# Transformer attention software-pipelined by the order of issue: scores of unit i+2 ahead of the values and sums of unit i

## The chip, the cores and the metric

One core of one Trainium2 chip runs the whole program. The metric is the device time of one execution in microseconds (us). A profile of one execution stands beside the timed runs. In it PE is TensorE's matmuls, PEld its weight loads, DVE is VectorE, ACT ScalarE, SP the queue that issues transfers. The ends of matmuls are modelled, so I read distances between starts ("pitches") rather than lengths. The granted clock is the share of TensorE's full speed that the profile shows as granted; 1.00 is full.

## The reference, cut to what matters

Two graph-attention layers, then one transformer layer on 4096 rows of 256 features, 8 heads of 32, with a 4096 x 4096 adjacency of 0 and 1 as mask. Only the attention of the last layer is touched:

```python
scores = jnp.einsum('nhd,mhd->hnm', q, k) * SCALE
scores = jnp.where(mask, scores, -jnp.inf)
attn = jax.nn.softmax(scores, axis=-1)
out = jnp.einsum('hnm,mhd->nhd', attn, v).reshape(n, DIM)
```

The kernel computes exp(scores) x mask without a shift, sums values and weights, and divides at the end; a flag would start a safe version if a sum left a wide range.

## The kernel before

A "unit" is one block of 512 query columns (nb), one half of the heads (c, four heads) and one tile of 128 keys (mt): 8 x 2 x 32 = 512 units. `HC` is 4, `O` 32, `NT` 32, `NB` 512, `MC` 8. I call the tiles `u_ps` score tiles (they lie in PSUM, where PE writes) and the tiles `u_e` weight tiles; a "turn" is the time from the first score of one unit to the first score of the next. In the traces, scores read `feat_a` and `feat_b`, the names of the tiles behind `q_t` and `k_t`.

```python
masks = tile_pool("u_masks", bufs=5);  work = tile_pool("u_work", bufs=6)
tail = tile_pool("u_tail", bufs=2)
ps_s = tile_pool("u_ps_s", bufs=3, space=PSUM)      # 2 banks each
ps_a = tile_pool("u_ps_a", bufs=1, space=PSUM)      # u_av, u_dn: 1 bank each
for nb in range(NNB):
    for k in range(NT // MC):                       # mask: load, turn into 0 and 1
        b = masks.tile([P, MC, NB], BF, name="u_mask")
        nc.sync.dma_start(b, v_cols[nb, :, k * MC : (k + 1) * MC, :])
        nc.vector.tensor_scalar(b, b, 0.0, None, op0=ALU.not_equal)
        ...
    for c in range(DC):
        av, dn = ...
        for mt in range(NT):
            ps = [ps_s.tile([P, 2, NB], F32, name="u_ps") for _ in range(HC // 2)]
            for j in range(HC):                     # scores: four row groups of the array
                nc.tensor.matmul(ps[j // 2][:, j % 2, :], k_t[...], q_t[...])
            for u in range(HC // 2):
                e = work.tile([P, 2, NB], F32, name="u_e")
                nc.scalar.activation(e, ps[u], AF.Exp)
                nc.vector.tensor_tensor(e, e, mask, op=ALU.mult)
            for to, left in ((av, None), (dn, ones)):
                for j in range(HC):                 # values, then sums: four column groups
                    nc.tensor.matmul(to[j * O : (j + 1) * O, :], ..., es[j // 2][:, j % 2, :],
                                     start=(mt == 0), stop=(mt == NT - 1))
        nc.scalar.copy(num, av);  nc.vector.tensor_copy(den, dn)
        ...                                         # store den
        nc.vector.reciprocal(inv, den)
        nc.vector.tensor_tensor(q_t[:, c, cols], num, inv, op=ALU.mult)
```

A scheduler that runs before the program is built fixes the order of instructions on each engine; it may differ from the order of the source.

## Time and profile before

| | before |
|---|---|
| timed median, 3 runs | 11645.31 us (11637.78 to 11648.66) |
| profiled span | 11641.4 us |
| attention stage, from its first scores to its last values and sums | 3494.5 us, 6.83 us a unit |
| granted PE clock in this stage | 0.90 |

The prediction below shows the slices (each digit the busy tenths of one fortieth of the span), the stage's window, its waits (engine and line, what it waited for, us in total, times, longest) and one turn of the timeline (start, length, engine, instruction; in square brackets the idle time before it and what ended it). What to see: no engine is full, and three waits recur in every unit. That is a ring.

### The profile page before, as it was taken

To read this page: it belongs to the slowest core of one execution; us is meant where nothing else is said; L and a number is where in the kernel's file an instruction comes from. 1 tells how busy PE (TensorE), PEld (TensorE's weight loads), DVE (VectorE), ACT (ScalarE), POOL (GpSimd) and SP (SyncE) were. 2 spreads that over 40 slices of the span, in tenths; PEclk is the share of its full clock that TensorE was granted. 3 is DMA by queue.
4 is the path that set the end of the run, shared out by engine and by line. 5 is a ranking of instruction groups with operands and counts; after the bars stand their busy time and mean duration, and the time that the engine had idled before them with its cause. 6 is when DMAs were issued, how large, how long until landed. Compare 5 with 4: busy or idle time off the path is not lost.

```text
span 11641.4 us, 101805 instructions
## 1 busy us (share of the span) xinstructions
PE 9711.6 (83%) x40040; PEld 3205.0 (28%) x40546; DVE 7718.6 (66%) x8204; ACT 5333.2 (46%) x7825; POOL 36.1 (0%) x47
## 2 busy tenths in 40 slices
PE   7888999999999888899999999966666666666669
PEld 4333322222222333332222222221111111111125
DVE  7999877777777899977777777733333333333331
ACT  1101288888888100038888888822222222222221
POOL 0000000000000000000000000000000000000000
PEclk8999999999999899999999999989988988988989
DMA  3232100000000100000000000000000000000000
GB/s 96 80 81 79 47 15 15 15 15 14 12 11 4 49 26 29 29 4 17 17 17 17 17 17 11 7 18 8 8 15 8 8 15 8 8 15 8 4 16 22
DMA packets 116850, 262.66 MB, mean 23 GB/s; under 512 B 12933, under 2 KB 87942, under 8 KB 91782
## 3 DMA queue, kind: packets, MB, share of 16 engines
q1 hardware_dynamic: 111750, 222.46, 5.5%
q0 software_dynamic: 4608, 33.56, 1.5%
q8 instruction: 319, 5.23, 0.2%
q14 instruction: 173, 1.42, 0.0%
HBM read 213.92 MB, written 75.50 MB: 25 GB/s over the span
## 4 chain that ended last, share of the span: by engine, by line
PE 62%; DVE 24%; ACT 6%; issue 6%; DMA 1%; SPq 0%; DVEq 0%; ACTq 0%; POOLq 0%
PE av L185 20%; DVE part L170 14%; PE u_av L859 9%; PE ps L375 8%; PE ps L382 7%; PE u_dn L859 7%; DVE u_e L852 5%; PE u_ps L840 5%; ACT u_e L850 4%; DVE e L405 2%; PE misc L359 2%; PE misc L949 1%; PE misc L935 1%; DMA v<-in_adj_dram 1%; ACT e L408 1%
## 5 line engine op out<-in xcount | busy, mean ns | idle before, releaser
L408 ACT ACTIVATE e<-e,terms 128x512 f32<-128x512 f32 x4096 | 2627.2, 709 | 458.3 <-DVE e L405 448.3
L405 DVE TENSOR_TENSOR e<-e,ps 128x1024 f32<-128x1024 f32 x2048 | 2450.3, 1218 | 274.2 <-PE ps L382 172.4
L852 DVE TENSOR_TENSOR u_e<-u_e,u_mask 128x1024 f32<-128x1024 f32 x1024 | 1208.0, 1221 | 2146.0 <-ACT u_e L850 2145.9
L185 PE MATMUL av<-e,v_sb 128*64 128x512 f32 x8192 | 2547.6, 617 | 52.7 <-ACT e L408 47.9
L170 DVE TENSOR_REDUCE part<-ps_peak 128x2 f32<-128x1024 f32 x2048 | 2328.2, 1216 | 69.5 <-PE ps_peak L274 63.5
L859 PE MATMUL u_av<-u_e,u_v 128*32 128x512 f32 x4096 | 1254.9, 781 | 1158.2 <-DVE u_e L852 1158.2
L850 ACT ACTIVATE u_e<-u_ps 128x1024 f32<-128x1024 f32 x1024 | 990.7, 1021 | 2448.9 <-PE u_ps L840 2448.9
L375 PE MATMUL ps<-bias,ident 128*128 128x512 bf16 x4084 | 1557.6, 381 | 186.8 <-DVE e L405 160.6
L390 ACT ACTIVATE e<-slope,steep 128x512 f32<-128x512 f32 x2048 | 1405.8, 712 | 343.4 <-PE av L185 335.5
L397 DVE TENSOR_SCALAR e<-slope,steep 128x512 f32<-128x512 f32 x2048 | 969.6, 483 | 792.6 <-PE av L185 756.1
L167 PE MATMUL ps_peak<-v,ident 128*128 128x512 bf16 x3997 | 1223.0, 386 | 292.7 <-DVE v L148 104.5
L382 PE MATMUL ps<-shift,select 128*128 128x512 bf16 x3784 | 1441.4, 381 | 1.6 <-issue 1.4
L274 PE MATMUL ps_peak<-dst_rows,select 128*128 128x512 bf16 x4013 | 1223.6, 385 | 5.9 <-issue 0.4
L859 PE MATMUL u_dn<-u_e,u_ones 128*32 128x512 f32 x4096 | 1140.2, 683 | 0.0
L185 PEld LDWEIGHTS av<-e,v_sb 128*64 128x64 f32 x8192 | 554.9, 134 | 1089.6 <-ACT e L408 983.6
L382 PEld LDWEIGHTS <-select 128*128 128x128 bf16 x4096 | 398.1, 97 | 1231.5 <-issue 975.6
L375 PEld LDWEIGHTS <-ident 128*128 128x128 bf16 x4096 | 398.5, 97 | 1149.7 <-issue 905.4
L167 PEld LDWEIGHTS <-ident 128*128 128x128 bf16 x4096 | 393.8, 99 | 994.6 <-issue 666.0
L840 PE MATMUL u_ps<-feat_a,feat_b 32*128 32x512 f32 x4096 | 617.3, 639 | 5.9 <-ACT u_e L850 5.4
L859 PEld LDWEIGHTS u_av<-u_e,u_v 128*32 128x32 f32 x4096 | 162.7, 120 | 1653.3 <-DVE u_e L852 1581.3
L289 ACT COPY stage<-pv 128x1024 bf16<-128x1024 bf16 x128 | 129.2, 1013 | 1041.5 <-PE pv L288 1041.5
L134 ACT COPY shift<-pr 17x1024 bf16<-17x1024 bf16 x8 | 7.6, 1000 | 1203.0 <-PE pr L133 1202.8
(132 smaller groups left out, 3734.4 us busy)
## 6 DMA issues: line engine op xcount, KB each, us to landing
bias<-v_cols SPq DMA_DIRECT2D x64, 1024.0 KB, 4.9
v<-in_adj_dram POOLq DMA_DIRECT2D x32, 1024.0 KB, 7.7
v_rows<-v SPq DMA_DIRECT2D x32, 1024.0 KB, 3.8
v_cols<-stage SPq DMA_DIRECT2D x16, 2048.0 KB, 8.9
v<-v_rows SPq DMA_DIRECT2D x32, 1024.0 KB, 4.8
u_mask<-v_cols SPq DMA_DIRECT2D x32, 1024.0 KB, 4.8
feat_b<-in_x_dram SPq DMA_DIRECT2D x8, 512.0 KB, 8.0
x_spill<-feat_a SPq DMA_DIRECT2D x8, 512.0 KB, 3.0
```

The lines of the kernel that those rows point to most:

```text
L167: nc.tensor.matmul(ps[:, j, :], ident, v[:, cols], start=True, stop=False)
L170: nc.vector.tensor_reduce(part[:, 2 * hp : 2 * hp + 2, w], ps, AX.X, ALU.max)
L185: nc.tensor.matmul(av[2 * O * j : 2 * O * (j + 1), :], v_sb[:, mt, VW * (h // 2) + O * (h % 2) : VW * (h // 2) + O * (h % 2) + 2 * O], p, ...
L274: nc.tensor.matmul(ps, select[:, h, :], dst_rows[:, cols], start=False, stop=True)
L375: nc.tensor.matmul(ps[:, j, :], ident, chunks[mt // MC][:, mt % MC, :], start=True, stop=False,)
L382: nc.tensor.matmul(ps[:, j, :], select[:, h, :], shift[:, cols], start=False, stop=True,)
L390: nc.scalar.activation(e[:, j, :], slope[:, j, :], AF.Relu, bias=steep[:, mt, h : h + 1],)
L405: nc.vector.tensor_tensor(e, e, ps, op=ALU.add)
L408: nc.scalar.activation(e[:, j, :], e[:, j, :], AF.Exp, bias=terms[:, mt, H + h : H + h + 1],)
L850: nc.scalar.activation(e, ps[u], AF.Exp)
L852: nc.vector.tensor_tensor(e, e, mask.unsqueeze(1).to_broadcast([P, 2, NB]), op=ALU.mult)
L859: nc.tensor.matmul(to[j * O : (j + 1) * O, :], v_sb[:, mt, h * O : (h + 1) * O] if left is None else left[:, :O], es[j // 2][:, j % 2, :], ...
```

## The change

The intent is to break the ring without another buffer or instruction. The loop body is split in two. `weights` issues a unit's scores, exponentials and mask products; `weigh` issues its values and sums. Two units of scores stay ahead.

```diff
-                for mt in range(NT):
-                    ps = [...]            # scores, exponentials, products
-                    ...
-                    for to, left in ((av, None), (dn, ones)):   # values and sums, same unit
-                        ...
+        def weights(nb, c, mt):           # scores, exponentials, products
+            if c == 0 and mt == 0:
+                load_masks(nb)
+            ...
+            return es
+        def weigh(nb, c, mt, es):         # values and sums; after mt == NT - 1 the division
+            ...
+        units = [(nb, c, mt) for nb in range(NNB) for c in range(DC) for mt in range(NT)]
+        pending = []
+        for unit in units:
+            pending.append((*unit, weights(*unit)))
+            if len(pending) > 2:
+                weigh(*pending.pop(0))
+        for unit in pending:
+            weigh(*unit)
```

More of the change, by code (lines that the diff above doesn't have):

```diff
@@ L825, in unshifted_transformer, with block_cols, load_masks @@
         ps_a = scope.enter_context(tc.tile_pool(name="u_ps_a", bufs=1, space=PSUM))
-        for nb in range(NNB):
-            cols = slice(nb * NB, (nb + 1) * NB)
+        masks_of = {}
+        sums_of = {}
+        def block_cols(nb):
+            return slice(nb * NB, (nb + 1) * NB)
+        def load_masks(nb):
             chunks = []
@@ L833, in unshifted_transformer @@
                 chunks.append(b)
-            for c in range(DC):
-                av = ps_a.tile([P, NB], F32, name="u_av")
-                dn = ps_a.tile([P, NB], F32, name="u_dn")
-                for mt in range(NT):
-                    ps = [ps_s.tile([P, 2, NB], F32, name="u_ps") for _ in range(HC // 2)]
-                    for j in range(HC):
-                        nc.tensor.matmul(
-                            ps[j // 2][:, j % 2, :],
-                            k_t[j * O : (j + 1) * O, c, mt * P : (mt + 1) * P],
-                            q_t[j * O : (j + 1) * O, c, cols],
-                            start=True,
-                            stop=True,
-                        )
-                    es = []
-                    for u in range(HC // 2):
-                        e = work.tile([P, 2, NB], F32, name="u_e")
-                        nc.scalar.activation(e, ps[u], AF.Exp)
-                        mask = chunks[mt // MC][:, mt % MC, :]
-                        nc.vector.tensor_tensor(
-                            e, e, mask.unsqueeze(1).to_broadcast([P, 2, NB]), op=ALU.mult
-                        )
-                        es.append(e)
-                    for to, left in ((av, None), (dn, ones)):
-                        for j in range(HC):
-                            h = c * HC + j
-                            nc.tensor.matmul(
-                                to[j * O : (j + 1) * O, :],
-                                v_sb[:, mt, h * O : (h + 1) * O] if left is None else left[:, :O],
-                                es[j // 2][:, j % 2, :],
-                                start=(mt == 0),
-                                stop=(mt == NT - 1),
-                            )
-                num = tail.tile([P, NB], F32, name="u_num")
-                den = tail.tile([P, NB], F32, name="u_den")
-                nc.scalar.copy(num, av)
-                nc.vector.tensor_copy(den, dn)
-                for j in range(HC):
-                    at = (nb * DC + c) * HC + j
-                    nc.sync.dma_start(dens[at : at + 1, :], den[j * O : j * O + 1, :])
-                inv = tail.tile([P, NB], F32, name="u_inv")
-                nc.vector.reciprocal(inv, den)
-                nc.vector.tensor_tensor(q_t[:, c, cols], num, inv, op=ALU.mult)
@@ new lines, in load_masks @@
+            masks_of[nb] = chunks
+        def weights(nb, c, mt):
+            if c == 0 and mt == 0:
+                load_masks(nb)
+            ps = [ps_s.tile([P, 2, NB], F32, name="u_ps") for _ in range(HC // 2)]
+            for j in range(HC):
+                nc.tensor.matmul(
+                    ps[j // 2][:, j % 2, :],
+                    k_t[j * O : (j + 1) * O, c, mt * P : (mt + 1) * P],
+                    q_t[j * O : (j + 1) * O, c, block_cols(nb)],
+                    start=True,
+                    stop=True,
+                )
+            es = []
+            mask = masks_of[nb][mt // MC][:, mt % MC, :]
+            for u in range(HC // 2):
+                e = work.tile([P, 2, NB], F32, name="u_e")
+                nc.scalar.activation(e, ps[u], AF.Exp)
+                nc.vector.tensor_tensor(
+                    e, e, mask.unsqueeze(1).to_broadcast([P, 2, NB]), op=ALU.mult
+                )
+                es.append(e)
+            return es
@@ new lines, in weigh @@
+        def weigh(nb, c, mt, es):
+            if mt == 0:
+                sums_of[nb, c] = (
+                    ps_a.tile([P, NB], F32, name="u_av"),
+                    ps_a.tile([P, NB], F32, name="u_dn"),
+                )
+            av, dn = sums_of[nb, c]
+            for to, left in ((av, None), (dn, ones)):
+                for j in range(HC):
+                    h = c * HC + j
+                    nc.tensor.matmul(
+                        to[j * O : (j + 1) * O, :],
+                        v_sb[:, mt, h * O : (h + 1) * O] if left is None else left[:, :O],
+                        es[j // 2][:, j % 2, :],
+                        start=(mt == 0),
+                        stop=(mt == NT - 1),
+                    )
+            if mt < NT - 1:
+                return
+            num = tail.tile([P, NB], F32, name="u_num")
+            den = tail.tile([P, NB], F32, name="u_den")
+            nc.scalar.copy(num, av)
+            nc.vector.tensor_copy(den, dn)
+            for j in range(HC):
+                at = (nb * DC + c) * HC + j
+                nc.sync.dma_start(dens[at : at + 1, :], den[j * O : j * O + 1, :])
+            inv = tail.tile([P, NB], F32, name="u_inv")
+            nc.vector.reciprocal(inv, den)
+            nc.vector.tensor_tensor(q_t[:, c, block_cols(nb)], num, inv, op=ALU.mult)
```

## The prediction

> **What bounds the kernel now.** I read, in this order: the slices of the span, the chain that ended last, the waits, and the timeline of single units. The slices show three stages with different limits:
>
> ```profile
> PE   7888999999999888899999999966666666666669
> ...
> DVE  7999877777777899977777777733333333333331
> ACT  1101288888888100038888888822222222222221
> ...
> PEclk8999999999999899999999999989988988988989
> ```
>
> The last third (about slice 27 to 39) is the transformer's attention, the only code that the change touches. No engine is full there: PE 6 tenths, DVE 3, ACT 2. A stage without a full engine is bound by a chain. The window that covers it alone gives its size:
>
> ```profile
> 7770.00:11264.50 3494.50, 2330.44 (x12288) 617.26 (x12288) 1311.47 (x1101) 1001.40 (x1042) 0.16 (x1) 0.90 0.03 10
> ```
>
> The columns are length, then busy time of PE, PEld, DVE, ACT and POOL, then granted clock. The stage has 512 units (8 column blocks x 2 halves x 32 key tiles), so one costs 3494.5 / 512 = 6.83 us, with only 2.56 us of DVE and 1.96 us of ACT. The waits of this window name the ring:
>
> ```profile
> ACT u_e L850 <- PE u_ps L840: 2448.9, 496, 9.4
> DVE u_e L852 <- ACT u_e L850: 2145.9, 481, 6.1
> ...
> PE u_av L859 <- DVE u_e L852: 1158.2, 495, 2.4
> ```
>
> Nearly every unit has all three waits. The timeline shows one turn of the ring (start, length, engine):
>
> ```profile
> 8001.20 1.14 PE L840 MATMUL u_ps<-feat_a,feat_b 32*128 32x512 f32 x8
> 8002.36 1.94 ACT L850 ACTIVATE u_e<-u_ps 128x1024 f32<-128x1024 f32 x2 [9.36 <-PE u_ps L840]
> 8003.41 2.36 DVE L852 TENSOR_TENSOR u_e<-u_e,u_mask 128x1024 f32<-128x1024 f32 x2 [6.07 <-ACT u_e L850]
> 8004.69 0.19 PEld L859 LDWEIGHTS u_av<-u_e,u_v 128*32 128x32 f32 x4 [3.18 <-DVE u_e L852]
> ```
>
> Scores end, ACT starts; ACT's first half ends, DVE starts; DVE's first half ends, the weighted values start, 8004.69 - 8001.20 = 3.49 us after the scores. Then come values and sums, and only then the next scores. In the chain of waits, two successive score starts are 6.47 us apart (9005.66 and 9012.13), a turn with PE at full speed; the value groups at 9001.65 and 9009.08 are 7.43 apart, a turn with slower matmuls. 6.83 lies between.
>
> **What the Trainium skill says.** "PSUM — Partial Sum Buffer", section Engine vs sequencer instructions: matmuls start and complete in program order, and the other engines' queues are strict first in, first out. So a score matmul that stands behind values waiting for DVE waits too, even with a free buffer. The trace agrees: PE sits idle 2.35 us before the values of most units. "TensorE: Matmul & The Clock Gate", section The mechanism: matmuls on different row or column groups of the array run concurrently. The trace agrees: eight sum matmuls of 592 ns each pass in 0.97 us. Same page, section What's actually happening: the array drops to half clock after an idle window of some 3.4 us. The trace agrees roughly: sum matmuls range from 592 to 1062 ns, and the mean clock is 0.90 although the idle stretch seen at PE is only 2.35 us.
>
> **The change, part by part.** It removes no instruction and adds none: 512 x (8 score, 8 value, 8 sum matmuls, 2 exponentials, 2 mask products). It only moves. The built order shows what the scheduler made of it. Before, PE's order in the steady part is 4 scores, 2 values, 1 sum, 2 values, 3 sums, all of one unit (each counted instruction there appears twice in the trace). After, it is 12 scores, then 4 values, 4 sums, 4 scores without exception: two units of scores always stand ahead. So a unit's values come two PE periods after its scores instead of right behind them.
>
> *Buffers.* Scores use 3 tiles, 2 per unit. The second tile of unit i+2 needs the first exponential of unit i+1, whose scores were issued a whole period earlier and whose exponential needs about 1 us: free in time. Weights have 6 tiles, three units: the exponentials of unit k need the values and sums of k-3 to be done, which stand before the scores of k in PE's order. Free too. Pool sizes are unchanged and suffice.
>
> *New bound, PE.* The trace of before holds short stretches in which scores were ready early by chance. At the first block's half boundary:
>
> ```profile
> 7998.29 1.12 PE L840 MATMUL u_ps<-feat_a,feat_b 32*128 32x512 f32 x2
> ...
> 7999.34 1.06 PE L859 MATMUL u_av<-u_e,u_v 128*32 128x512 f32 x8
> ...
> 8000.23 1.04 PE L859 MATMUL u_dn<-u_e,u_ones 128*32 128x512 f32 x8
> ...
> 8001.20 1.14 PE L840 MATMUL u_ps<-feat_a,feat_b 32*128 32x512 f32 x8
> ```
>
> Starts give pitches: 8000.23 - 7999.34 = 0.89 for 8 values and 8001.20 - 8000.23 = 0.97 for 8 sums. The score group there is a partial one; a full one of 8 lasts 1.14 with the pipeline's end, and the chain counts 1.06 of it. Sum 1.06 + 0.89 + 0.97 = 2.92 us. A second stretch, 7785.37 to 7791.16, has pitches of 2.90 and 2.89 at granted clock 1.00, but with half units. I take **2.92**; 512 x 2.92 = 1495 us.
>
> *DVE and ACT beside it.* DVE back to back takes 3.49 us for 3 products, 1.16 each. Per 32 units: 64 x 1.16 = 74.2, one denominator copy 0.69, one reciprocal 3.35, one product 0.68, two mask conversions 2.44: 81.4 us, against 32 x 2.92 = 93.4 of PE: 87%. ACT: 2 x 0.97 = 1.94 per unit, 66%. The ring's latency from scores to both masked tiles is 1.16 + 1.05 + 2.36 = 4.57 us; the values are due 2 x 2.92 + 1.06 = 6.90 us after the scores' start. **Slack 2.3 us.**
>
> *What stays exposed: the 15 inner boundaries between halves.* Value and sum accumulators have one buffer each, so the next half's first values wait until ACT and DVE have copied them. Let the scores that precede the last values start at 0. These values and sums end at 2.92; DVE, which stands at the products of two units later, is free at 4.6, copies until 5.3; the next values would have started at 2.92 + 1.06 = 3.98. Stall 1.4. Then the reciprocal delays the products of the next unit until 11.7, needed at 11.2: 0.5 more. 1.9 x 15 = 28 us. The 3.35 us reciprocal exceeds the slack, but DVE regains over 0.5 us per unit.
>
> *Start.* The first values cannot start before the first mask's transfer and conversion, 7.5 us into the stage as now; four more conversions (1.22 each) between the first products delay units 1 to 4. I put the end of the fifth unit at 23.5 us into the stage. Then 507 x 2.92 = 1480, plus 28, less two score groups at the end, 2.1: **1530 us**.
>
> *Sum.* The other stages are untouched: 11641.4 - 3494.5 = 8146.9. Plus 1530 is 9677 for the profiled span; the timed median of before lies 4 us above its span. I add some 10 us for waits at changes of matmul kind that I have not seen. **9690 us**, 16.8% less.
>
> **Rivals.** (a) *DVE becomes the bound.* Were the products paced at their listed mean of 1.22 plus a 0.04 issue gap, a half would cost 64 x 1.26 + 7.2 = 87.8 us, still below 93.4. It needs 1.35 us a product to bind; only contention unseen here does that. (b) *A buffer wait replaces the one removed*: three score tiles hold one and a half units. If scores had to wait for the second exponential of the unit before, the period would be about 1.14 + 1.94 plus hand-overs, near 3.2, so some 9830. The tile rotation speaks against it. (c) *PE runs faster than the stretch shows*: three groups at 0.89 would be 2.67, so 9560. The sums' 0.97 and the scores' 1.06 recur, at a change of shape, so I doubt it. (d) *The clock stays throttled at 0.90*: 2.92 / 0.90 = 3.24, so 9850. The gaps that the slow clock follows go away, and the page's other stages hold 0.98 with PE over 90% busy, so 1.00 to 0.98 is likelier. (e) *Nothing happens*, because the scheduler reorders back: excluded by the built order.
>
> **Range and chances.** Each 0.01 us of period is 5 us. I believe in 2.87 to 3.05 for it and 10 to 60 us for boundaries together: 9640 to 9780. To miss 2% the period would have to be above 6.3. Faster 0.98.
>
> **What would show it right or wrong.** In the new profile, the attention's slices should show PE 9, DVE 8, ACT 6 to 7, PEclk 9. The waits of ACT for scores should fall from 2449 us to 300 to 600 (ACT idles because PE is full, some 0.9 us per unit), those of PE for DVE from 1158 to under 60. Score starts should be 2.9 us apart. The chain should be made of values, sums and scores on PE almost alone in this stage. It is wrong if PE shows recurring gaps before scores (buffers), if the products average over 1.3 us (contention), or if the granted clock stays near 0.9.

## The result, and the profile after

The changed kernel takes 9699.12 us (median of 4 runs, 9688.92 to 9707.96), against 11646.99 us for the kernel before in the same rounds. The ratio is 0.8328, 95% interval 0.8314 to 0.8343. A ratio here is the mean time of one kernel's fast runs over that of the other's of the same rounds, so not quite the ratio of the medians.

First the slices of the changed kernel, whose attention now is slices 33 to 38:

```profile
PE   7888899999999998888889999999999699999989
...
DVE  7999987777777776999996777777877488888851
ACT  1111138888888886000007888888888266666641
PEclk8999999999999998999999999999999899999999
```

PE has nines in place of sixes, DVE eights in place of threes, ACT sixes in place of twos. The window of the stage (length; busy PE, PEld, DVE, ACT, POOL; clock):

```profile
7769.57:9321.50 1551.93, 1530.66 (x12286) 382.65 (x12288) 1301.37 (x1101) 1002.05 (x1042) 0.00 (x0) 0.99 0.07 23
```

The stage went from 3494.5 to 1551.9 us: 1942.6 of the 1942.9 us by which the profiled span shrank. DVE's and ACT's busy times are within 1% of those before (1311 and 1001 us), so no work went away. The waits in the changed stage, from 7780 us on, that is without its start:

```profile
ACT u_e L858 <- PE u_ps L847: 545.6, 509, 5.6
...
DVE u_e L859 <- ACT u_e L858: 189.6, 354, 0.6
DVE u_mask L837 <- DMA u_mask<-v_cols: 54.1, 27, 2.2
...
PE u_dn L875 <- DVE u_den L887: 17.9, 15, 2.8
...
PE u_av L875 <- DVE u_e L859: 1.4, 9, 0.2
```

PE's wait for DVE fell from 1158 us to 1.4. ACT and DVE now wait because PE paces them; of the chain of work in this stage, 89% is scores, values and sums on PE, as foretold (65% before). Two waits are new: the mask's conversion on DVE waits for its transfer (before, only once, at the start, for 7.6 us), and the first sums of a half wait for DVE's copy of the denominator. The timeline of one steady unit:

```profile
8501.07 1.14 PE L847 MATMUL u_ps<-feat_a,feat_b 32*128 32x512 f32 x8
...
8502.14 1.06 PE L875 MATMUL u_av<-u_e,u_v 128*32 128x512 f32 x8
...
8503.02 1.04 PE L875 MATMUL u_dn<-u_e,u_ones 128*32 128x512 f32 x8
...
8503.99 1.14 PE L847 MATMUL u_ps<-feat_a,feat_b 32*128 32x512 f32 x8
```

Pitches: 1.07 for scores, 0.88 for values, 0.97 for sums, together 2.92. Of the 511 turns, 456 are 2.9 us. Of the other 55, 4 are at the start, 30 at the boundaries between halves, and 21 inside second halves: three in each block but the last, 3.1 to 3.4 us long, each just after DVE has waited some 2 us for a mask's transfer. These 21 waits and one at each of six boundaries are the 27 of the table. The worst kind of boundary, between two column blocks:

```profile
7968.61 1.14 PE L847 MATMUL u_ps<-feat_a,feat_b 32*128 32x512 f32 x8
...
7969.21 1.23 DVE L837 TENSOR_SCALAR u_mask<-u_mask 128x4096 bf16<-128x4096 bf16 x1 [1.86 <-DMA u_mask<-v_cols]
...
7970.36 2.35 DVE L859 TENSOR_TENSOR u_e<-u_e,u_mask 128x1024 f32<-128x1024 f32 x2
7972.63 0.68 DVE L887 COPY u_den<-u_dn 128x512 f32<-128x512 f32 x1
...
7973.37 1.93 PE L875 MATMUL u_dn<-u_e,u_ones 128*32 128x512 f32 x8 [2.62 <-DVE u_den L887]
7975.23 1.91 PE L847 MATMUL u_ps<-feat_a,feat_b 32*128 32x512 f32 x8
```

DVE stands at a conversion whose transfer has not landed. Everything behind it on DVE is late: two products, then the copy of the denominator, on which the next half's sums wait 2.62 us. The turn takes 6.62 us instead of 2.92 (7968.61 to 7975.23), and the one after it 3.69 (to 7978.92).

### The profile page after: what moved, and what is told of

The parts are those of the page before. It is cut to its first block, busy times and chain, and to the rows that moved or that the text cites. A ratio compares the mean times of both kernels' runs of the same rounds, so it can differ in the third digit from the quotient of the medians.

```text
span 9698.5 us, 102325 instructions
## 1 busy us (share of the span) xinstructions
PE 8964.8 (92%) x40546; PEld 2965.1 (31%) x40546; DVE 7707.9 (79%) x8204; ACT 5334.2 (55%) x7825; POOL 36.2 (0%) x47
## 4 chain that ended last, share of the span: by engine, by line
PE 66%; DVE 23%; issue 6%; ACT 2%; DMA 2%; SPq 0%; DVEq 0%; ACTq 0%; POOLq 0%
PE av L185 24%; DVE part L170 17%; PE ps L375 10%; PE ps L382 9%; PE u_ps L847 5%; PE u_av L875 5%; PE u_dn L875 4%; DVE e L405 2%; PE misc L359 2%; PE misc L977 1%; PE misc L963 1%; DMA v<-in_adj_dram 1%; PE misc L797 1%; ACT e L390 1%; DVE u_e L859 1%
## 5 line engine op out<-in xcount | busy, mean ns | idle before, releaser
L382 PE MATMUL ps<-shift,select 128*128 128x512 bf16 x4096 | 1561.6, 381 | 0.0
L167 PE MATMUL ps_peak<-v,ident 128*128 128x512 bf16 x4096 | 1242.9, 385 | 280.4 <-DVE v L148 103.7
L382 PEld LDWEIGHTS <-select 128*128 128x128 bf16 x4096 | 398.1, 97 | 1231.8 <-issue 976.1
L847 PE MATMUL u_ps<-feat_a,feat_b 32*128 32x512 f32 x4096 | 591.6, 645 | 2.1 <-ACT u_e L858 1.6
L875 PE MATMUL u_dn<-u_e,u_ones 128*32 128x512 f32 x4096 | 551.8, 596 | 17.9 <-DVE u_den L887 17.9
L875 PE MATMUL u_av<-u_e,u_v 128*32 128x512 f32 x4096 | 565.3, 608 | 1.4 <-DVE u_e L859 1.4
L274 PEld LDWEIGHTS <-select 128*128 128x128 bf16 x4096 | 400.9, 98 | 506.8 <-issue 34.7
```

What stands on the lines that cost most here:

```text
L167: nc.tensor.matmul(ps[:, j, :], ident, v[:, cols], start=True, stop=False)
L274: nc.tensor.matmul(ps, select[:, h, :], dst_rows[:, cols], start=False, stop=True)
L382: nc.tensor.matmul(ps[:, j, :], select[:, h, :], shift[:, cols], start=False, stop=True,)
L847: nc.tensor.matmul(ps[j // 2][:, j % 2, :], k_t[j * O : (j + 1) * O, c, mt * P : (mt + 1) * P], q_t[j * O : (j + 1) * O, c, block_cols(nb) ...
L875: nc.tensor.matmul(to[j * O : (j + 1) * O, :], v_sb[:, mt, h * O : (h + 1) * O] if left is None else left[:, :O], es[j // 2][:, j % 2, :], ...
```

## The experiments

Each kernel is an edit of the changed kernel and was timed against the kernel before. All gave correct results but the one that says otherwise. The changed kernel is at ratio 0.8328. The diffs are cut to the lines that matter.

**1. Lead 0.**

```diff
-            if len(pending) > 2:
+            if len(pending) > 0:
```

> The changed code with a lead of 0 units: the values of a unit are issued right behind its own scores, as before the change. Theory (the lead alone makes the gain): back at the time of the kernel before, 11647 us within 20, attention stage about 3494 us, granted clock there 0.90. Rival (the rewriting itself, such as the later masks or the other grouping, makes part of the gain): clearly below 11647, say 11400 or less.

Measured: 11654.66 us, ratio 1.0003 (0.9988 to 1.0018). The steady PE order is that of the kernel before again. The rewriting alone makes no difference clear of noise; the lead makes the gain.

**2. Lead 1.**

```diff
+            if len(pending) > 1:
```

> Lead of 1 unit. Theory (the lead must cover the latency from scores to both masked tiles, 4.6 us): with one unit ahead the second product is still in flight when its values are due, so two periods take 4.6 + 0.86 + 0.86 = about 6.4 us, 3.2 us a unit; stage about 1690 us, total about 9845 (9800 to 9900). Rival (any lead hides the latency): 9700 as with lead 2. Rival (one unit is not enough to break the ring): over 10500.

Measured: 9945.57 us, ratio 0.8539. That is 45 us above the theory's range and far from both rivals. The timeline shows the steady state as expected:

```profile
8501.84 1.14 PE L847 MATMUL u_ps<-feat_a,feat_b 32*128 32x512 f32 x8
8502.91 1.27 PE L875 MATMUL u_av<-u_e,u_v 128*32 128x512 f32 x6
...
8504.01 0.60 PE L875 MATMUL u_av<-u_e,u_v 128*32 128x512 f32 x2
...
8505.40 1.14 PE L847 MATMUL u_ps<-feat_a,feat_b 32*128 32x512 f32 x8
8506.47 1.06 PE L875 MATMUL u_av<-u_e,u_v 128*32 128x512 f32 x8
```

Six value matmuls go and the last two come 1.1 us later, when the second product is done. This turn takes 3.56 us, the next 2.93, in alternation: 3.24 on average, as worked out (3.2). What my sum left out is boundaries: 512 x 3.24 = 1659, while the stage took 1795 us. That leaves 136 us for start and boundaries, where the changed kernel has 54 (1552 less 1498). With no slack, turns at boundaries last up to 11 us instead of up to 6.6, and the 21 turns after mask conversions 5.4 to 5.8 us instead of 3.1 to 3.4. So the second unit of lead is worth 0.31 x 512 = 161 us in steady units and some 80 at boundaries and conversions, about half of that at conversions.

**3. Lead 3, same buffers.**

```diff
+            if len(pending) > 3:
```

> Lead of 3 units with the same 6 weight tiles and 3 score tiles. Theory (the lead of 2 is what the buffers carry): the exponential of a unit must wait for the values and sums of three units earlier, which now stand behind its own scores, and the next scores then wait for that exponential: about 1.0 us more a unit, total about 10220 (10000 to 10400). Rival (a longer lead always helps or is neutral): 9670 to 9700.

Measured: 10247.85 us, ratio 0.8801. The timeline:

```profile
8501.06 2.31 PE L847 MATMUL u_ps<-feat_a,feat_b 32*128 32x512 f32 x8
8501.16 1.94 ACT L858 ACTIVATE u_e<-u_ps 128x1024 f32<-128x1024 f32 x2 [2.15 <-PE u_dn L875]
...
8505.15 2.31 PE L847 MATMUL u_ps<-feat_a,feat_b 32*128 32x512 f32 x8
```

ACT waits for sums (u_dn), that is for a weight tile to come free, no longer for scores; and score groups stretch to 2.31 us because they wait for that exponential. The turn is 4.09 us. The lead must fit the buffers.

**4. Lead 3 with 8 weight tiles.** Room for two more came from the small tiles at a half's end.

```diff
-work = tile_pool("u_work", bufs=6);  tail = tile_pool("u_tail", bufs=2)
+work = tile_pool("u_work", bufs=8);  tail = tile_pool("u_tail", bufs=1)
-            nc.vector.reciprocal(inv, den)
-            nc.vector.tensor_tensor(q_t[...], num, inv, op=ALU.mult)
+            nc.vector.reciprocal(out_q, den)          # out_q = q_t[:, c, block_cols(nb)]
+            nc.vector.tensor_tensor(out_q, num, out_q, op=ALU.mult)
```

with `len(pending) > 3`.

> Lead of 3 with 8 weight tiles; to make room the three small tiles at the end of a half have one buffer and the reciprocal is written straight to its destination. Theory (PE is full in the steady part, only boundaries are left): period again 2.92, the late products after a boundary vanish, 20 to 25 us less than the changed kernel, 9675 (9660 to 9695). Rival (the buffers are not what made the lead of 3 slow): as slow as the lead of 3 with 6 tiles.

Measured: 9682.37 us, ratio 0.8311 (0.8300 to 0.8322). Turns of 2.9 us rise from 456 to 488. The stage is 1527.5 us, 25 less than with lead 2. The buffers were what made experiment 3 slow, and more slack helps only at boundaries and after conversions: the 21 turns of 3.1 to 3.4 us are gone.

**5. Two score tiles, two of each accumulator.**

```diff
-ps_s = tile_pool("u_ps_s", bufs=3);  ps_a = tile_pool("u_ps_a", bufs=1)
+ps_s = tile_pool("u_ps_s", bufs=2);  ps_a = tile_pool("u_ps_a", bufs=2)
```

> Score tiles 3 to 2, and the two accumulators get a second buffer each with the freed banks (lead 2). Theory (three score tiles are just enough: with two, the second scores tile of a unit needs the second exponential of the unit before, which in the trace ends 0.2 us after these scores start): 0.2 to 0.3 us more a unit, 100 to 150 us, less about 20 to 30 at the boundaries where the sums no longer wait for the copy: 9700 + 90 = 9790 (9740 to 9850). Rival (the third tile is slack): 9670. Rival (scores must wait for whole exponentials): over 9850.

Measured: 9746.95 us, ratio 0.8367. Within the range, though nearer its low end: turns alternate between 2.9 and 3.1 to 3.2 us, 3.04 on average, as the score groups show:

```profile
8500.95 1.37 PE L847 MATMUL u_ps<-feat_a,feat_b 32*128 32x512 f32 x8
...
8504.11 1.14 PE L847 MATMUL u_ps<-feat_a,feat_b 32*128 32x512 f32 x8
...
8507.03 1.37 PE L847 MATMUL u_ps<-feat_a,feat_b 32*128 32x512 f32 x8
```

Every other group waits 0.2 us for an exponential. The third tile is just enough and worth more than a second accumulator. What the second accumulator alone is worth cannot be split off in this run.

**6. No mask conversions.** The adjacency of this input is 0 or 1 already, so the result stays right for it, but not for any other nonzero number.

```diff
-                nc.vector.tensor_scalar(b, b, 0.0, None, op0=ALU.not_equal)
```

> The 32 conversions of masks to 0 and 1 on DVE are left out (the adjacency of this input is 0 or 1 already, so the result stays right). In the trace after the change 27 of them made DVE wait for the mask transfer, 54 us together, up to 2.2 us each. Theory (this new wait is most of what the stage lost against the prediction: 1552 measured, 1530 predicted): boundaries between column blocks fall from about 4.5 us to about 1.6, the other waits vanish: 25 to 35 us less, 9665 to 9675. Rival (it is hidden anyway): 9699, within 8.

Measured: 9682.54 us, ratio 0.8315 (0.8304 to 0.8327), 17 us less by the medians; the total missed the expected 9665 to 9675 by 8 us. In the profile the stage fell from 1552 to 1528 us, 24 less, just under the 25 to 35 that were expected. The runs of the changed kernel differ by up to 19 us, and among the profiles here (experiment 8 aside) the start of the attention by 22 us, so the stage is the better measure, though from one profile each. The same block boundary now reads:

```profile
7968.94 1.14 PE L846 MATMUL u_ps<-feat_a,feat_b 32*128 32x512 f32 x8
...
7971.26 1.06 PE L874 MATMUL u_dn<-u_e,u_ones 128*32 128x512 f32 x8 [0.19 <-DVE u_den L886]
7972.26 1.14 PE L846 MATMUL u_ps<-feat_a,feat_b 32*128 32x512 f32 x8
```

3.32 us instead of 6.62, and all 15 boundaries are alike: one turn of 3.3 and one of 4.1. The 21 longer turns inside second halves are gone as well. The conversions made both. The run takes away their work (1.2 us each) as well as their wait (1.9 us in the case shown), so it does not split the two. I tried two other cures without a run: moving the conversion to its first use in the source (the scheduler put it back in the same place) and giving it to GpSimd (the build refused that comparison there).

**7. Without the sums.** Sums only for the first key tile; the denominator gets 1 added so that nothing divides by zero. Its output is wrong, which doesn't matter for the time.

```diff
+                if to is dn and mt > 0:
+                    continue
-                        stop=(mt == NT - 1),
+                        stop=(mt == NT - 1 or to is dn),
-            nc.vector.tensor_copy(den, dn)
+            nc.vector.tensor_scalar(den, dn, 1.0, None, op0=ALU.add)
```

> Wrong on purpose: the sums' matmuls run only for the first of the 32 key tiles (the sum plus one stands in for the denominator), which takes 0.97 of 2.92 us off PE. Theory (PE is the bound after the change, DVE is next with 1.16 a product): the period falls to DVE's 2.33 us plus its boundary work, stage 16 x 82 = 1312 plus 15, total about 9475 (9450 to 9520). Rival (the ring through the buffers still paces it, PE is busy but not the bound): 9650 to 9700. Rival (DVE already binds): 9690.

Measured: 9515.93 us, ratio 0.8171, at the upper end of the range. The window of the stage's middle:

```profile
7900.00:9100.00 1200.00, 1091.74 (x7362) 272.16 (x7360) 1123.82 (x974) 883.46 (x921) 0.00 (x0) 0.96 0.07 24
```

DVE is at 94% (1123.8 of 1200) and PE at 91% with its clock down to 0.96. In this window the chain runs over DVE's mask products for 75% of its time. Less work on PE makes the stage shorter, until DVE is nearly full: PE was the bound after the change, and DVE stood close behind.

**8. Lead 0 with filler matmuls.** Six bf16 matmuls on constants after each unit's scores, into a PSUM bank that nothing reads; score tiles 3 to 2 to free it.

```diff
+            for _ in range(6):
+                nc.tensor.matmul(warm, fill[:, :P], fill, start=True, stop=True)
```

> Lead 0 (as before the change), with 6 matmuls on constant bf16 data after each unit's scores, into a bank of their own that nothing reads; they fall into the time in which PE waited, and score tiles are 2 so that a bank is free. Theory (part of the cost of a unit before was the half clock that PE falls to after its idle stretches: 6.47 us a turn at full clock, 6.83 in the mean): the granted clock rises from 0.90 to about 1.0, stage 512 x 6.47 = 3313 us, total about 11465 (11430 to 11530). Rival (the clock has no part in it): 11647 or slower.

Measured: 11590.77 us, ratio 0.9950 (0.9935 to 0.9965). The total missed the expectation by 126 us. The windows of the kernel before and of this one:

```profile
7800.00:11200.00 3400.00, 2264.24 (x11952) 599.76 (x11952) 1273.69 (x1070) 973.11 (x1012) 0.00 (x0) 0.90 0.03 9
```

```profile
7800.00:11200.00 3400.00, 2861.95 (x15060) 809.21 (x15315) 1310.03 (x1099) 1000.07 (x1040) 0.00 (x0) 0.99 0.03 11
```

The clock did rise from 0.90 to 0.99, and the steady turns did become full-speed ones: 457 take 6.5 us, where before 288 did and 189 took 7.3 to 7.6. But the stage only fell from 3494 to 3409 us. With two score tiles the boundaries cost more (two units in 15.4 to 16.7 us, where before three fitted into 19.6), turns with a mask conversion last 7.6 to 8.9 us, and in this kernel the stages ahead of it took 35 us longer (it starts 17 us later than in any other profile here), for a reason I did not find.

The clock records of the kernel before show the clock's part turn by turn: in each of the 288 turns of 6.5 us it was 1.00 throughout, and in each of the 189 longer ones it was at one half for 3.4 us. Two turns in a row:

```profile
8998.16:9005.59 7.43, 5.08 (x26) 1.41 (x25) 2.36 (x2) 1.94 (x2) 0.00 (x0) 0.77 0.00 0
9005.59:9012.06 6.47, 4.12 (x26) 1.06 (x24) 2.36 (x2) 1.94 (x2) 0.00 (x0) 1.00 0.00 0
```

The busy time of DVE and ACT is the same in both; PE's is not. So the clock's share is shown per turn, not in the total: the mean of these 477 turns was 6.84, 0.37 above a full-speed one. An estimate from that is 0.37 x 512 = 190 us, a tenth of what the change gained.

**9. Lead 3, 8 weight tiles, no conversions.** The edits of 4 and 6.

> Lead 3 with 8 weight tiles and no mask conversions: both boundary remedies together. Theory (PE is full; start 15 us, 512 x 2.925 = 1498, only the sums' wait for the copied accumulator is left, 0.4 us at 15 boundaries): stage about 1517, total about 9665 (9655 to 9680), 34 us less than the changed kernel, and no way to go lower without less work on PE. Rival (the two remedies act on the same waits and don't add): 9682 as each alone.

Measured: 9654.67 us, ratio 0.8291 (0.8280 to 0.8303). A window of the stage:

```profile
7900.00:9200.00 1300.00, 1297.58 (x10628) 321.82 (x10620) 1097.74 (x927) 864.95 (x899) 0.00 (x0) 1.00 0.07 23
```

PE is busy 99.8% of it; 492 of 511 turns are 2.93 us, 15 are 3.3 and 4 are at the start. The stage is 1510 us, of which 512 x 2.925 = 1498. The two remedies add (17 us each alone; 44 together, where 34 was expected, so the total is 0.3 us under the range), and after the start only the sums' wait of 0.4 us at 15 boundaries is left.

**10. bf16 weights and values.** In the changed kernel.

```diff
-v_sb = vals.tile([P, NT, D], F32, name="u_v");   e = work.tile([P, 2, NB], F32, name="u_e")
+v_sb = vals.tile([P, NT, D], BF, name="u_v");    e = work.tile([P, 2, NB], BF, name="u_e")
-            for to, left in ((av, None), (dn, ones)):
+            for to, left in ((av, None), (dn, ones_b)):       # ones in bf16
```

> Lead 2 as changed, but the weights, the values and the ones are bf16, so values and sums are one pass of PE instead of two; scores stay fp32. Theory (PE was the bound; now ACT is next, its exponentials follow each other every 0.92 to 0.97 us, 1.84 to 1.94 a unit): stage 512 x 1.9 + about 40 = 1010, total about 9160 (9120 to 9260), if DVE's product gets faster in bf16; if it stays at 1.16 us, DVE binds at 2.33 a unit and the total is about 9475. Rival (the order of issue is all there was to gain): 9700. The result stays within tolerance.

Measured: 9255.52 us, ratio 0.7949 (0.7937 to 0.7962), correct, at the upper end of the range. Values and sums pass at 0.2 to 0.3 us a group, and the product on DVE fell from 1.22 to 0.69 us. The median turn is 2.02 us, and the stage took 1100 us where the theory had 1010.

**11. The same with lead 3, 8 weight tiles, 8 mask tiles.**

> The same with lead 3, 8 weight tiles and 8 mask tiles, which fit as bf16 halves the values and the weights. With a shorter period (about 1.9) a lead of 2 covers 2 x 1.9 + 1.1 = 4.9 us, hardly more than the latency of 4 to 4.6. Theory: where lead 2 leaves waits for the products, lead 3 takes them away: 20 to 60 us less than lead 2 in bf16, more at the boundaries. Rival (ACT is full already): within 15 us of it.

Measured: 9183.14 us, ratio 0.7891 (0.7879 to 0.7903), 72 us less than experiment 10, a little more than the 20 to 60 expected. The window:

```profile
7900.00:8750.00 850.00, 829.63 (x6760) 292.26 (x6759) 643.41 (x907) 806.01 (x859) 0.00 (x0) 0.98 0.08 27
```

ACT is at 95% (806 of 850), and PE by its records at 98% (830), with score groups stretched from 1.14 to 1.35 us and more. Which of the two paces the other no run here separates. Nor does one split the 72 us among the lead, the weight tiles and the mask tiles; that a shorter period asks for a longer lead is the idea, not shown by itself. This version beats both kernels.

## Why the prediction was right

**The bound before (a ring, not an engine).** Right. Experiment 1 brings the ring back with the changed code; the waits shrink as foretold (PE for DVE to 1.4 us, under 60 foretold; ACT for PE to 546, foretold 300 to 600).

**The new bound and its period.** Right: 2.92 foretold from a chance stretch of the old trace, 2.92 measured. Experiment 7 shows that PE paces it, and in 9 PE is full and the turns are the same.

**Slack and buffers.** Right. Experiments 2 and 3 bracket the lead: one unit is too little for the second product, three too much for six weight tiles; 5 shows that three score tiles are just enough. The rival of a buffer wait fell for these sizes only.

**Clock and the other rivals.** 0.99 was granted in the stage, so (d) fell. The products still average 1.22 us, so nothing contends and (a) fell. The pitches of scores and sums recur at every turn, so (c) fell. In experiment 1 the old order is back with the old time, so (e) fell with it.

**The boundaries.** This step failed in part: a term was mis-sized, in both directions. The start was right (end of the fifth unit at 23.7 us, foretold 23.5). Inside a block I put 1.4 + 0.5 = 1.9 us. The trace has 0.40 (7872.64 to 7875.96 against 2.92) and then 1.19 (7878.89 to 7883.00), 1.6 in all. The first part was too large because only the sums wait for DVE's copy; the values wait for ACT's, which ends 1.6 us earlier (7873.31 against 7874.91). The second was too small. Between blocks I missed a mechanism: I counted the mask conversions as DVE work but not as a place in a strict queue where DVE waits for a transfer. It made six of the seven block boundaries cost 4.4 to 4.6 us (3.70 + 0.77 in the case shown) instead of 1.9; the seventh, where DVE stands at no conversion, cost 1.6. The same waits inside second halves, where I had put nothing, stretched 21 turns, by 6.4 us together. The sum is 6 x 4.5 + 9 x 1.6 + 6.4 = 48 us where I had 28. The stage came to 1552 us instead of 1530, and experiment 6 takes 24 us back by removing the conversions. The 10 us that I added "for waits at changes of matmul kind" hid half of the miss; that the total came within 9 us was luck to that extent, for no such waits exist beyond the pitches.

**What the Trainium skill said.** "PSUM — Partial Sum Buffer", section Engine vs sequencer instructions, in-order matmuls and strict queues elsewhere: this carried the whole argument, and would have shown the mask wait too, had I applied it to DVE: two products and the copy stand behind a conversion that waited 1.86 us. "TensorE: Matmul & The Clock Gate", section The mechanism, concurrent groups: agrees, the instructions of a group start four at a time, within 0.02 us, and eight pass in 0.88 to 1.07 us. On the clock I wrote that the trace "agrees roughly"; it shows the half clock, but no idle stretch of 3.4 us (see the last section). "Perfetto Trace Analysis", section Optimization Strategy, says that the same gap recurring on the engine that should be saturated can mean too few buffers for the next tile. Experiment 3 is such a case: 1.16 us more in every unit, gone with two more tiles in 4.

## What to carry to other kernels

When no engine is full and the waits form a ring, order the in-order engine so that work that is ready stands ahead of work that waits. The lead must be long enough for the ring's latency to the *last* piece a unit needs (4.6 us at a period of 2.9 asked for two units, not one) and short enough for the buffers. The old trace can hold a few turns in which the overlap happened by chance; their pitches foretell the new period. Afterwards look at the boundaries, and at anything that waits for a transfer inside a strict queue.

## What the Trainium skill lacked or had wrong

- "TensorE: Matmul & The Clock Gate", section What's actually happening, ties the half clock to an idle window of some 3.4 us. In the kernel before, the idle stretch seen at PE was 2.35 us in each turn of 6.5, and the clock still fell to one half 204 times, for 3.4 us each, so that its mean was 0.90; with fillers that left 0.97 us idle the mean was 0.99. The same page's section "A second HAM failure mode: psum-queue depth-cycling" tells of short idle times that make the clock oscillate, but gives no length; this is one measured pair.
- No page gives the pitch of fp32 matmuls on four groups where the kind of group changes (it would belong to "TensorEngine Tiling (Array Packing)", section Key Properties, which tells of a drain at a change of mode without its length): 1.07 us from scores on row groups to values on column groups, 0.88 from values to sums on the same column groups, 0.97 from sums back to scores.
- "Perfetto Trace Analysis", section Optimization Strategy, names too few buffers as a cause of a recurring gap. A lead that is too long for the buffers gives the same picture (4.09 us a turn at lead 3, 2.93 at lead 2 with the same tiles), and there the cure can be to shorten the lead.
